# A graph layer on one core: what the scatters of a slot wait for

## The chip, the core and the metric

The kernel runs on one core of a Trainium2 chip. The core has five engines with an instruction stream each: TensorE (PE in the profile; PEld is its weight load), VectorE (DVE), ScalarE (ACT), GpSimd (POOL) and SyncE (SP). They work in order, each on its own stream, and wait for one another by semaphores. Sixteen DMA engines move data between the device memory and the on-chip memories; SP and POOL issue nearly all of this kernel's transfers.

The metric is the time of one execution on the device, in microseconds (us). The kernel before takes 1373.15 us (median of three runs, 1372.46 to 1373.16).

## The reference

There are 6250 nodes with 128 features each and 100,000 edges, sorted by their `dst` node. Each edge builds a message from its two nodes and its own features, the messages are summed at the edge's `src` node, and the result is added to the node and normalized:

```python
def layer(x, edge_index, edge_attr, W, b, gamma, beta):
    row, col = edge_index[0], edge_index[1]          # src, dst
    msg_in = concatenate([x[row], x[col], edge_attr], axis=-1)
    h = msg_in @ W + b
    mu = mean(h, axis=-1, keepdims=True)
    var = mean(square(h - mu), axis=-1, keepdims=True)
    h = (h - mu) * rsqrt(var + 1e-05) * gamma + beta
    msg = relu(h)
    return segment_sum(msg, row, num_segments=x.shape[0])
x = layernorm(x + layer(x, stack([src, dst]), edge_attr_128, W, b, gamma, beta))
```

Edges come sorted by `dst`, and are summed by `src`. The kernel therefore has to reorder them.

## The kernel before, in words

**Tiles, slots and splits.** The edges are cut into 782 tiles of 128. Four tiles make a slot, so there are 196 slots (`q`). The tiles are also cut into five splits (`SPLITS`), of 164, 168, 168, 164 and 118 tiles. The nodes are cut into 50 blocks by `src`, two of which make a pair: 25 pairs per split.

**The first half of the work: a slot.** `edges` (L520 to L534) makes four products of edge features with their part of `W` in float32 (`hp<-w,eT`, L529) and adds the `dst` node's part by four products with a one-hot matrix (`hp<-win,ohd`, L533). `evict` copies the result from PSUM to one of eight row buffers `hs` on ScalarE (L541, L542). `scatters` (L548 to L571) then sends the rows of each tile to a place in device memory by an indirect DMA from GpSimd (L559), such that the rows of one node block lie together (`sorted`). The places come from `places`, a counting sort on VectorE and TensorE (L372 to L444), worked some slots ahead.

**The second half: a pair.** When a split has been scattered, its pairs are loaded (`hl<-sorted`, L612) and go through a chain: one-hot of the block's node on VectorE (`ohe`, L630), its transposes on TensorE (L642), eviction on ScalarE (`ohn`, L646), the `src` node's part by products (`sel`, L669) on top of what ScalarE seeded (L652), squares and root on ScalarE (L678, L681), reciprocal and scaling on VectorE (L687, L693), the sum by node as float32 products (`pa`, L702), and the addition to the accumulator on VectorE (L710).

**Order.** The streams of TensorE, VectorE, ScalarE and SyncE are written out by hand: what the Python program issues first stands first. GpSimd's is left to a scheduler. The main loop goes over the slots. In a slot it issues the one-hot of slot q+2 (`edge_hot`), the products of slot q, the pair steps that are due (`work`, 100 pairs of four steps each over the slots after the first split), the eviction of slot q and the steps of `places`. The last split's pairs come after the loop (`tail`), with the final normalization.

**What paces the scatters.** In slots 13 to 194 (`TIE`), the call near the end of slot q scatters the four tiles of slot q-1 that are still in `waiting`. Each is tied to a product of slot q: `pe` has logged the products since the last call with a cost (4 for a float32 one, 1 for another), the list's total is cut in four, and the k-th scatter waits for the product in which the k-th quarter ends. Before slot 12 and after slot 194 a scatter waits for no product, only for its rows and places. All scatters go through GpSimd's queue in order, and each takes one of eight semaphores, so that it also waits for the landing of the scatter eight before it.

**Who waits for scatters.** The eviction of slot q writes the row buffer of slot q-8 and waits for that slot's four scatters to land. The pair loads of a split wait for all of its scatters. There is a second, general path behind a flag, for inputs of another shape; it isn't taken here.

## Time and profile before

| what | value |
|---|---|
| median of three runs | 1373.15 us |
| the profiled execution's own time | 1371.87 us |
| its span in the trace | 1370.07 us |
| mean granted TensorE clock | 0.857 |
| TensorE busy | 962.5 us (70%) |
| VectorE busy | 876.2 us (64%) |
| GpSimd busy | 839.3 us (61%) |
| ScalarE busy | 731.1 us (53%) |
| first and last scatter (L559) start | 24.6 us, 1224.1 us |

How to read it: busy time counts the instructions of an engine that do work, not its waits. The chain of waits follows the execution back from its last instruction, and books each stretch to the engine that was then being waited for; an engine with a small share of the chain can be busy and still not set the end. "issue" is time in which nothing that the profile shows was being waited for, and "remote" is a wait whose releaser isn't seen. The ends of TensorE's products are modelled, so a wait for one can seem to end after the product did. [...]

### The profile page before, as it was taken

What the parts mean: (1) busy time and instruction counts of PE and PEld (TensorE: products, weight loads), DVE (VectorE), ACT (ScalarE), POOL (GpSimd) and SP (SyncE); (2) the same over time, 40 slices, a digit from 0 to 9 for tenths busy, and PEclk for the clock granted to TensorE, in tenths of its full rate; (3) what the DMA queues carried; (4) which work ended last, traced back from release to release, by engine and by line L of the source; (5) the groups of instructions that cost most, each with busy time, mean ns of one, the idle gap of its engine ahead of it and who ended that gap; (6) DMA issues with size and microseconds to landing.
All of it is one profiled execution on the core that took longest, in us unless ns stands there. A gap on an engine that the chain in (4) does not pass through costs nothing.

```text
span 1370.1 us, 27285 instructions
## 1 busy us (share of the span) xinstructions
PE 962.5 (70%) x8721; PEld 857.8 (63%) x8721; DVE 876.2 (64%) x2411; ACT 731.1 (53%) x3054; POOL 839.3 (61%) x899
## 2 busy tenths in 40 slices
PE   3645555245777777777778676776877888878995
PEld 3545544235766676666667676676767777767884
DVE  8764543425566565757676665657567766657996
ACT  1222221114565555555655556555655788777996
POOL 3666667666666666666666666666666666550664
PEclk9767776566989888999998889879899999999998
DMA  6867764355656654657655554667645665532552
GB/s 199 239 200 226 223 211 145 126 169 176 204 181 209 201 172 144 189 183 217 202 183 177 182 167 157 215 192 214 212 143 183 191 187 191 168 112 92 158 162 74
DMA packets 122273, 245.78 MB, mean 179 GB/s; under 512 B 46555, under 2 KB 60396, under 8 KB 122118
## 3 DMA queue, kind: packets, MB, share of 16 engines
q1 hardware_dynamic: 95956, 189.83, 46.0%
q0 software_dynamic: 25184, 53.31, 11.0%
q8 instruction: 70, 1.15, 0.3%
q10 hardware_dynamic: 978, 0.80, 0.2%
q14 instruction: 85, 0.70, 0.2%
HBM read 155.74 MB, written 88.11 MB: 178 GB/s over the span
## 4 chain that ended last, share of the span: by engine, by line
PE 45%; issue 19%; DVE 15%; ACT 12%; another core or an unknown queue 7%; DMA 2%; POOL 0%; ACTq 0%; DVEq 0%; POOLq 0%
PE pa L702 12%; PE hp L529 12%; PE sel L669 11%; ACT sq L678 4%; PE tr L642 3%; PE hp L533 3%; DVE sc L389 3%; PE beside L426 3%; DVE msg L693 2%; DVE ohe L630 2%; ACT ohn L646 2%; ACT sel L652 2%; ACT fsq L748 1%; ACT hs L541 1%
## 5 line engine op out<-in xcount | busy, mean ns | idle before, releaser
L559 POOL DMA_INDIRECT sorted<-hs,place_i x782 | 771.8, 987 | 434.7 <-issue 196.5
L529 PE MATMUL hp<-w,eT 128*128 128x128 f32 x1564 | 276.3, 321 | 80.9 <-issue 59.1
L678 ACT ACTIVATE sq<-sel 128x128 f32<-128x128 f32 x875 | 230.8, 280 | 178.8 <-remote 62.7
L541 ACT COPY hs<-hp 128x512 f32<-128x512 f32 x196 | 114.3, 583 | 358.5 <-issue 143.5
L669 PE MATMUL sel<-xa,ohn 128*128 128x128 bf16 x2625 | 217.2, 231 | 124.2 <-issue 65.2
L702 PE MATMUL pa<-msg,ohe 128*128 128x130 f32 x1900 | 281.5, 299 | 30.5 <-issue 24.0
L669 PEld LDWEIGHTS <-ohn 128*128 128x128 bf16 x2850 | 194.0, 103 | 166.1 <-issue 150.2
L529 PEld LDWEIGHTS hp<-w,eT 128*128 128x128 f32 x1564 | 238.6, 227 | 94.5 <-issue 71.2
L702 PEld LDWEIGHTS pa<-msg,ohe 128*128 128x128 f32 x1900 | 254.7, 210 | 43.9 <-issue 36.9
L693 DVE SCALAR_TENSOR_TENSOR msg<-sel,rstd,cut 128x128 f32<-128x128 f32 x875 | 247.1, 345 | 8.7
L678 ACT ACTIVATION_READ_ACCUMULATOR sq<-sel 128x1 f32 x875 | 183.9, 210 | 0.0
L630 DVE TENSOR_TENSOR ohe<-hl,beside 128x1024 f32<-128x1024 f32 (+1 forms) x125 | 144.5, 1156 | 50.1 <-remote 19.0
L646 ACT COPY ohn<-tr 128x1024 bf16<-128x1024 bf16 (+1 forms) x125 | 120.1, 961 | 27.8 <-remote 11.1
L710 DVE TENSOR_TENSOR acc<-acc,pa 128x260 f32<-128x260 f32 x100 | 42.3, 423 | 138.5 <-remote 44.9
L517 DVE TENSOR_SCALAR ohd<-db,part_w 128x512 bf16<-128x512 bf16 x194 | 70.3, 363 | 85.2 <-remote 53.6
L652 ACT COPY sel<-hl 128x512 f32<-128x512 f32 x200 | 118.8, 594 | 1.5 <-DVE msg L693 1.5
L533 PE MATMUL hp<-win,ohd 126*128 126x128 bf16 x782 | 93.4, 241 | 29.8 <-issue 28.2
L642 PE MATMUL tr<-ident_h,ohe 128*128 128x128 bf16 x950 | 84.0, 228 | 31.4 <-issue 28.5
L533 PEld LDWEIGHTS <-ohd 126*128 126x128 bf16 x782 | 71.1, 111 | 41.3 <-issue 36.7
L642 PEld LDWEIGHTS <-ohe 128*128 128x128 bf16 x950 | 63.7, 102 | 38.7 <-issue 38.0
L687 DVE RECIPROCAL rstd<-std 128x4 f32<-128x4 f32 (+1 forms) x250 | 43.0, 172 | 65.8 <-ACT std L681 46.4
L681 ACT ACTIVATE std<-ss,eps 128x4 f32<-128x4 f32 (+1 forms) x250 | 74.4, 298 | 8.1
(159 smaller groups left out, 874.6 us busy)
## 6 DMA issues: line engine op xcount, KB each, us to landing
hl<-sorted SPq DMA_DIRECT2D x100, 528.0 KB
eT<-in_eT SPq DMA_DIRECT2D x96, 512.0 KB
sorted<-empty SPq DMA_DIRECT2D x125, 198.0 KB
db<-drel_d SPq DMA_DIRECT2D x96, 256.0 KB
sorted<-hs,place_i POOLq DMA_INDIRECT x782
hl<-sorted SPq DMA_DIRECT2D x25, 396.0 KB
win<-xb_d SPq DMA_DIRECT2D x196, 31.5 KB
xb_d<-xb SPq DMA_DIRECT2D x16, 384.0 KB
```

The lines of the kernel that those rows point to most:

```text
L529: pe(nc.tensor.matmul(hp[:, j, :], eT[:, at], w[:, 2, :], start=j == 0, stop=False, skip_group_check=True), 4)
L533: pe(nc.tensor.matmul(hp[:, j, :], oh[:3 * WN, at], win[:3 * WN, :], start=False, stop=j == m - 1, skip_group_check=True))
L541: nc.scalar.copy(hs[:, :m, 0:D], hp[:, :m, :])
L559: i = nc.gpsimd.indirect_dma_start(out=sorted_d[s][:, :], out_offset=bass.IndirectOffsetOnAxis(ap=place_i[:parts, t:t + 1], axis=0), in_=h ...
L630: nc.vector.tensor_tensor(self.ohe[:, :k, :], self.hl[:, :k, D:D + 1].to_broadcast([P, k, P]), row_bc(iota_p, k), op=ALU.is_equal)
L642: pe(nc.tensor.transpose(tr[:, j, :], half[:, j0 + j, 1::2], ident_h))
L646: nc.scalar.copy(self.ohn[:, :self.k, :], self.tr[:, :self.k, :])
L652: nc.scalar.copy(self.sel[g][:, :m, :], self.hl[:, j0:j0 + m, 0:D])
L669: pe(nc.tensor.matmul(sel[:, j, :], self.ohn[:, j0 + j, :], xa[:, b, i * D:(i + 1) * D], start=False, stop=j == m - 1 and i == 2, skip_gro ...
L678: nc.scalar.activation(sq[:, j, :], self.sel[g][:, j, :], AF.Square, accum_out=ss[:, j:j + 1])
L693: nc.vector.scalar_tensor_tensor(self.msg[:, j0 + j, 0:D], self.sel[g][:, j, :], rstd[:, j:j + 1], cut, op0=ALU.mult, op1=ALU.max)
L702: pe(nc.tensor.matmul(self.pa[:, h, :], self.ohe[:, j, :], self.msg[:, j, :], start=(j == h), stop=(j == k - 2 + h)), 4)
```

## The change

The ties keep their slots (13 to 194), their number (four) and the rows that they hold. What they hold them for changes. The log `done` no longer takes products with their cost; it takes every operation issued on VectorE, whichever step it belongs to, with a cost of its output columns plus 64. The k-th scatter of a call waits for the VectorE operation in which the k-th quarter of that total ends. To log them, all of the main path's VectorE operations are issued through a wrapper, `vec`, in place of `nc.vector`, and the products lose their `pe(...)`. Apart from the waits and signals, each engine's stream has the same instructions, and the four that are ordered by hand have them in the same order; on GpSimd, whose order the program's scheduler sets, five of the last ten scatters (those of the tiles of slots 193 and 194) change places.

```diff
     done = []
 
-    def pe(i, cost=1):
-        done.append((i.ins, cost))
-        return i
+    class Logged:
+        def __getattr__(self, name):
+            op = getattr(nc.vector, name)
+
+            def call(*args, **kw):
+                i = op(*args, **kw)
+                n = 1
+                for x in (kw["out"] if "out" in kw else args[0]).shape[1:]:
+                    n *= x
+                done.append((i.ins, n + 64))
+                return i
+
+            return call
+
+    vec = Logged()
...
         for j in range(m):
             at = slice(j * P, (j + 1) * P)
-            pe(nc.tensor.matmul(hp[:, j, :], eT[:, at], w[:, 2, :], start=j == 0, stop=False,
-                                skip_group_check=True), 4)
+            nc.tensor.matmul(hp[:, j, :], eT[:, at], w[:, 2, :], start=j == 0, stop=False,
+                             skip_group_check=True)
...
             if tied:
-                tc.add_manual_dep(i.ins, at[k].name, written, reason="rows behind products")
+                tc.add_manual_dep(i.ins, at[k].name, written, reason="rows behind VectorE's work")
...
-                nc.vector.scalar_tensor_tensor(self.msg[:, j0 + j, 0:D], self.sel[g][:, j, :],
+                vec.scalar_tensor_tensor(self.msg[:, j0 + j, 0:D], self.sel[g][:, j, :],
                                                rstd[:, j:j + 1], cut, op0=ALU.mult, op1=ALU.max)
...
-                nc.vector.tensor_tensor(acc[:, b:b + 2, :], acc[:, b:b + 2, :], self.pa,
+                vec.tensor_tensor(acc[:, b:b + 2, :], acc[:, b:b + 2, :], self.pa,
                                         op=ALU.add)
...
```

The lines left out are the same replacement, `vec` for `nc.vector` or a product without `pe`.

## The prediction, made before the changed kernel ran

> **What bounds the kernel now.** I read the page first: busy shares, chain, the groups of GpSimd and of the lines around it.

> ```profile
> PE 962.5 (70%) x8721; PEld 857.8 (63%) x8721; DVE 876.2 (64%) x2411; ACT 731.1 (53%) x3054; POOL 839.3 (61%) x899
> ...
> PE 45%; issue 19%; DVE 15%; ACT 12%; another core or an unknown queue 7%; DMA 2%; POOL 0%; ACTq 0%; DVEq 0%; POOLq 0%
> ...
> L559 POOL DMA_INDIRECT sorted<-hs,place_i x782 | 771.8, 987 | 434.7 <-issue 196.5
> ...
> L693 DVE SCALAR_TENSOR_TENSOR msg<-sel,rstd,cut 128x128 f32<-128x128 f32 x875 | 247.1, 345 | 8.7
> ```

> The scatters (L559) are 782 instructions of 987 ns, with 434.7 us of idle time before them. GpSimd holds 0% of the chain that ended last; it is TensorE, time that no shown wait explains, VectorE and ScalarE. The busy time by stage says where the scatters' engine has room:

> ```profile
> 320.00:560.00 240.00, 175.20 (x1608) 157.68 (x1607) 149.32 (x387) 133.76 (x561) 151.85 (x156) 0.85 0.60 188
> ...
> 800.00:1060.00 260.00, 195.15 (x1814) 177.05 (x1811) 170.65 (x440) 149.16 (x625) 164.51 (x169) 0.88 0.59 187
> 1060.00:1230.00 170.00, 135.21 (x1485) 126.27 (x1484) 111.63 (x337) 130.44 (x567) 103.17 (x106) 0.96 0.54 169
> ```

> Columns are the stretch, its length, busy time of PE, PEld, DVE, ACT and POOL, then TensorE's granted clock, DMA share and GB/s. From 320 to 560 us, 156 scatters at 0.97 us plus the 0.30 us that stands before even a back-to-back one need 198 of 240 us. So GpSimd has about a sixth of each slot to spare, and spends it on waits, listed here from 320 to 1230 us (line, releaser, total us, times, longest):

> ```profile
> POOL sorted L559 <- issue: 124.7, 371, 2.0
> POOL sorted L559 <- PE sel L669: 57.5, 56, 2.7
> POOL sorted L559 <- remote: 51.4, 39, 2.8
> POOL sorted L559 <- PE pa L702: 39.2, 39, 2.5
> ```

> The first row is mostly the 0.30 us (371 x 0.30 = 111 us). Taking 0.30 us off every start leaves 160 us in 182 waits after the 180th scatter. These are the ties to TensorE that the change removes.

> **What could make a scatter's time matter.** Three things wait for scatters. (a) The eviction (L541) reuses one of eight row buffers. I took each eviction's waits from the built program and the landing of those scatters from the DMA packets: the rows had left the buffer at least 23 us before the eviction started, in the median 35 us. (b) The pair loads of a finished split (L612). The last scatter of splits 0 to 3 lands 14.4, 18.4, 18.9 and 12.7 us before the first load is issued, by the same packets. (c) The last split, the tightest:

> ```profile
> 1224.11 0.87 POOL L559 DMA_INDIRECT sorted<-hs,place_i  x1 [0.30 <-issue]
> ...
> 1229.32 0.58 ACT L652 COPY sel<-hl 128x512 f32<-128x512 f32 x1
> ...
> 1229.92 0.32 SPq L612 DMA_DIRECT2D hl<-sorted  x1
> ```

> The last scatter lands at 1225.8. The load goes at 1229.92, just after ScalarE's copy out of its buffer ends at 1229.90, so it waits for the buffer. 4.1 us are spare, and its first reader (ohe, L630) runs at 1247.0.

> **The change part by part.**

> *Removed: ties of 728 scatters to products.* Of the 160 us of waits, none lies on the end's path by (a) to (c). Credit 0. If the cover were gone, the end would move by what the last scatter moves, at most.

> *Added: 605 scatters wait for a VectorE operation, 133 have no wait of their own.* One big operation (scan, one-hot) can hold two or more of the four quarter points. Behind a waiting scatter stand only the next scatters and, in the tail, the y operations; VectorE itself waits for no scatter except through a later split. Example, GpSimd first, then VectorE:

> ```profile
> 631.91 0.97 POOL L559 DMA_INDIRECT sorted<-hs,place_i  x1 [0.30 <-issue]
> 634.05 0.97 POOL L559 DMA_INDIRECT sorted<-hs,place_i  x1 [1.17 <-PE pa L702]
> 635.32 0.97 POOL L559 DMA_INDIRECT sorted<-hs,place_i  x1 [0.30 <-issue]
> 637.47 0.97 POOL L559 DMA_INDIRECT sorted<-hs,place_i  x1 [1.18 <-PE sel L669]
> ```

> ```profile
> 627.63 2.33 DVE L389 TENSOR_TENSOR_SCAN sc<-oh,beside 128x1050 bf16<-128x1050 bf16 x1
> 630.88 1.13 DVE L693 SCALAR_TENSOR_TENSOR msg<-sel,rstd,cut 128x128 f32<-128x128 f32 x4
> 633.94 0.42 DVE L710 TENSOR_TENSOR acc<-acc,pa 128x260 f32<-128x260 f32 x1 [1.93 <-PE pa L702]
> ```

> By the built program the scatter at 634.05 will wait for the scan that ended at 629.96, the next for the first L693 (631.23), the one at 637.47 for L710 (634.36). They could have gone at 633.2 (631.91 + 1.27), 634.5 and 635.7: 0.9 to 1.8 us earlier. I did this for all tied scatters, with VectorE's times as they stand and 0.25 us from release to start. After the 180th scatter the named operation had ended 2.8 us before the scatter's actual start in the median (5th and 95th percentiles 5.6 and 0.2 us); replayed in order, scatters start 1.5 us earlier in the median, never more than 2.1 us later, the last one 0.7 us earlier. GpSimd's waits come to 179 us in 168 places: the slack is moved, not removed. On the end's path: 0.7 us less of the 4.1 us spare in (c), which nobody waits for. Term 0; bounds -0.7 and 0 by this path alone.

> *Before about 320 us* neither kind of tie binds: GpSimd runs back to back behind the evictions. Term 0.

> *Signals.* TensorE instructions that signal fall from 1552 to 996; VectorE's rise from 1763 to 1855. Between 320 and 1215 us, start to start after an L693 is 258 ns without and 263 ns with a signal: 92 x 5 ns = +0.5 us if all were on the path. After an L669 product it is 56 ns either way: 556 x 0 = 0. [...]

> *GpSimd beside VectorE.* A scatter released by the end of one VectorE operation starts beside the next. 40 of 782 scatters lasted over 1.05 us, 14.2 us too long in all; of 28 that met the two-input L411, 14 are among them. If ten times as many met it, 142 us would still fit the 160 us of spare waits: term 0. [...]

> *Unknown: the phase between scatters and the rest of the DMA traffic.* TensorE has idle time with no releaser: 60.4 + 24.8 + 17.0 + 16.7 + 13.4 + 6.9 = 139.2 us "issue" from 320 to 1060 us. In microseconds where TensorE paused over 0.5 us so, 2.4 scatter packets were in flight against 1.8 otherwise, a weak link that may run either way. A scatter without a wait of its own can run on while TensorE pauses: 133 of 728, 18%, so at most 18% x 139 = 25 us lost. The other end: starts 1.5 us earlier taking as much off. I take 0, since the two kernels issue the same bytes at nearly the same mean spacing, and keep -12 and +13 (half of each) for the range.

> **Sum.** Profiled execution 1371.87 (span 1370.07 and 1.80 around it) + 0.5 = 1372.4. The median of the three runs stands 1.28 above that execution: 1373.6 us.

> **The rivals.**

> *Slower: scatters run on through TensorE's pauses.* Place: 320 to 1060 us. For it: the 139 us of unexplained pauses, the packet counts, and the ties to products stopping GpSimd exactly in such pauses (57.5 + 39.2 us of its waits). Against: VectorE starves in the same pauses a little later, and holds scatters then. Price 13 us: 1386. It decides from 2.7 us, which is 2% more pauses.

> *Faster: earlier landings release evictions.* The waits list has this row:

> ```profile
> ACT hs L541 <- DMA sorted<-hs,place_i: 42.4, 17, 5.0
> ```

> If these 17 waits were for landings, 1.5 us each would give 25 us, of which I price half as being on the chain: 12 us, 1361. Against: the program's evictions wait for scatters eight slots back, landed 23 us or more before; the last releaser seen is then a coincidence, and the product is the real one. [...]

> *No change in the order at all:* excluded as far as the program goes, since 605 waits differ; elsewhere every instruction keeps its place on its engine, but for five of the last ten scatters, which change places among themselves.

> **How the numbers follow.** Three runs span 0.7 us; 0.2% (2.7 us) is about what a measurement of this kernel tells from no change. No measurable change 0.40 (1371 to 1376), the slower rival 0.37, faster 0.23. The likeliest case's own range is 1371 to 1376. Eight in ten needs most of both rivals, whose prices are half of their bounds: 1362 to 1388 leaves out the outer tail of each, about 0.1 and 0.1. Point 1373.6.

> **What would show it.** Right: GpSimd's waits before scatters named after VectorE, about 160 to 190 us; scatters 1 to 2 us nearer to their slot; the last scatter at 1223 to 1226; busy times of all engines unchanged to 1%; the first load of the last split right after a ScalarE copy. Wrong: TensorE's "issue" time away from 139 us by over 3 us in that stretch, scatters lengthened far beyond 14 us in all, or an eviction that truly waits for a landing.

## The result, and the profile after

| | before | changed |
|---|---|---|
| median of four runs on the same chip | 1372.93 us (1372.46 to 1373.16) | 1482.7 us (1478.1 to 1490.2) |
| ratio, 95% interval | | 1.0805 (1.0756 to 1.0855) |
| span of the profiled execution | 1370.1 us | 1476.3 us |
| mean granted TensorE clock | 0.857 | 0.802 |

The change made the kernel 8% slower; 1373.6 us was forecast, within 1362 to 1388. These are lines of the changed kernel's page that answer to those shown of before: busy time, the granted clock in 40 slices, the chain that ended last, the scatters and ScalarE's squares. (Line numbers have moved by 14; L573 is the scatter. VectorE's operations all stand at L104, the wrapper's line.)

```profile
PE 1012.8 (69%) x8721; PEld 899.3 (61%) x8721; DVE 873.6 (59%) x2411; ACT 728.7 (49%) x3054; POOL 833.1 (56%) x899
...
PEclk9867676667777878786878888887787898988998
...
PE 42%; issue 21%; DVE 14%; ACT 11%; another core or an unknown queue 9%; POOL 1%; DMA 1%; SPq 0%; ACTq 0%; POOLq 0%; DVEq 0%
...
L573 POOL DMA_INDIRECT sorted<-hs,place_i x782 | 765.8, 979 | 547.0 <-issue 215.4
...
L692 ACT ACTIVATE sq<-sel 128x128 f32<-128x128 f32 x875 | 230.0, 280 | 241.0 <-remote 160.3
```

VectorE, ScalarE and GpSimd do the same work in the same time (within 1%). TensorE has the same 8721 products, but is busy 50 us longer, at a lower clock. GpSimd's share of the chain is 1%: late scatters are not what the others wait for. The stages show that the loss is everywhere in the loop (columns as in the prediction):

```profile
320.00:560.00 240.00, 165.16 (x1380) 146.12 (x1380) 131.42 (x337) 114.90 (x479) 134.87 (x139) 0.76 0.54 167
...
800.00:1060.00 260.00, 184.44 (x1642) 165.36 (x1641) 154.87 (x401) 133.77 (x569) 150.01 (x155) 0.82 0.54 169
```

In the same 240 us from 320 on, TensorE did 1380 products instead of 1608, at a clock of 0.76 instead of 0.85. What TensorE waited for, from 320 to 1060 us (line, releaser, total us, times, longest): before,

```profile
PE sel L669 <- issue: 60.4, 89, 1.9
PE tr L642 <- issue: 24.8, 32, 1.5
...
PE pa L702 <- issue: 16.7, 30, 1.1
```

and after:

```profile
PE sel L683 <- issue: 92.0, 119, 1.8
PE pa L716 <- issue: 38.8, 60, 1.7
PE tr L656 <- issue: 22.2, 34, 1.4
```

"issue" is time in which nothing that the profile shows was waited for. I call these **pauses**: over 0.25 us between two products of which the second waits for no semaphore. To compare kernels I take the loop by its work, from the first `sel` product to the last `hp` product, and split its length into pauses, waits, and the rest, which is TensorE working:

| us | loop | pauses | waits | rest | of the loop at half clock (0.5 in the trace's records of the granted clock) |
|---|---|---|---|---|---|
| before | 1037.0 | 135.9 | 90.7 | 810.4 | 204.8 |
| changed | 1139.5 | 215.1 | 65.5 | 858.8 | 389.1 |
| difference | +102.5 | +79.2 | -25.2 | +48.4 | +184.3 |

The loop explains 102.5 of the 106.2 us between the spans; the part before it is 3.9 us longer. So the loss is 79 us more pauses and 48 us of the same products run more slowly, less 25 us of waits. This count looks at the product's own waits; the weight load just ahead of it may still wait for a semaphore. Pauses where the weight load waits for nothing either I call **strict**: they are 124.6 us before and 198.9 us after, 74.3 us more.

GpSimd's waits after, from 320 to 1340 us, are named as forecast, and are longer because everything is:

```profile
POOL sorted L573 <- issue: 165.4, 408, 8.0
POOL sorted L573 <- DVE ohd L104: 120.4, 54, 6.3
POOL sorted L573 <- ACT hs L556: 35.2, 18, 4.2
POOL sorted L573 <- DVE rstd L104: 35.0, 33, 4.5
```

**One burst of pauses in each kernel.** Pauses come in bursts. In the timeline (start, length, engine, line, operation, count, idle time before it) this is one of before, TensorE first and GpSimd below:

```profile
380.87 0.61 PE L669 MATMUL sel<-xa,ohn 128*128 128x128 bf16 x5 [0.25 <-issue]
381.97 0.27 PE L669 MATMUL sel<-xa,ohn 128*128 128x128 bf16 x2 [0.49 <-issue]
383.38 0.27 PE L669 MATMUL sel<-xa,ohn 128*128 128x128 bf16 x2 [1.14 <-issue]
384.11 0.22 PE L669 MATMUL sel<-xa,ohn 128*128 128x128 bf16 x1 [0.45 <-issue]
384.81 0.27 PE L669 MATMUL sel<-xa,ohn 128*128 128x128 bf16 x2 [0.49 <-issue]
```

```profile
380.26 0.97 POOL L559 DMA_INDIRECT sorted<-hs,place_i  x1 [0.30 <-issue]
381.54 0.97 POOL L559 DMA_INDIRECT sorted<-hs,place_i  x1 [0.30 <-issue]
382.81 0.97 POOL L559 DMA_INDIRECT sorted<-hs,place_i  x1 [0.30 <-issue]
385.59 0.97 POOL L559 DMA_INDIRECT sorted<-hs,place_i  x1 [1.81 <-ACT hs L542]
```

and this one of the changed kernel:

```profile
494.68 0.22 PE L683 MATMUL sel<-xa,ohn 128*128 128x128 bf16 x1 [0.25 <-issue]
496.28 0.22 PE L683 MATMUL sel<-xa,ohn 128*128 128x128 bf16 x1 [1.39 <-issue]
497.69 0.22 PE L683 MATMUL sel<-xa,ohn 128*128 128x128 bf16 x1 [1.19 <-issue]
499.11 0.27 PE L683 MATMUL sel<-xa,ohn 128*128 128x128 bf16 x1 [1.20 <-issue]
500.51 0.27 PE L683 MATMUL sel<-xa,ohn 128*128 128x128 bf16 x1 [1.13 <-issue]
501.23 0.28 PE L683 MATMUL sel<-xa,ohn 128*128 128x128 bf16 x1 [0.46 <-issue]
502.64 0.28 PE L683 MATMUL sel<-xa,ohn 128*128 128x128 bf16 x1 [1.13 <-issue]
503.34 0.71 PE L683 MATMUL sel<-xa,ohn 128*128 128x128 bf16 x5 [0.42 <-issue]
```

```profile
494.02 0.97 POOL L573 DMA_INDIRECT sorted<-hs,place_i  x1 [0.30 <-issue]
495.29 0.96 POOL L573 DMA_INDIRECT sorted<-hs,place_i  x1 [0.30 <-issue]
496.56 1.03 POOL L573 DMA_INDIRECT sorted<-hs,place_i  x1 [0.30 <-issue]
497.90 0.96 POOL L573 DMA_INDIRECT sorted<-hs,place_i  x1 [0.30 <-issue]
499.17 0.97 POOL L573 DMA_INDIRECT sorted<-hs,place_i  x1 [0.31 <-issue]
500.44 0.97 POOL L573 DMA_INDIRECT sorted<-hs,place_i  x1 [0.30 <-issue]
504.32 0.97 POOL L573 DMA_INDIRECT sorted<-hs,place_i  x1 [2.91 <-DVE ohd L104]
```

Products of one accumulation group, which wait for nothing that the profile shows, come one or two at a time, 0.7 or 1.4 us apart, instead of every 56 ns (the median from one `sel` product to the next at full clock). Before, three scatters went out and the fourth started 1.81 us late, 0.8 us after TensorE was running again (the profile names ScalarE's L542 as what ended that wait). After, six scatters follow one another at GpSimd's shortest distance of 0.30 us until 501.41, in a burst of 8.7 us; the next waits until 504.32. The last pauses of the two bursts end 1.0 and 1.9 us after GpSimd had made its last scatter. Between 330 and 1060 us, GpSimd was making a scatter in 50% of the pause time before and in 68% after (at full clock; outside pauses 66% and 64%). Over all pauses of the loop, at either clock, it was 46% and 61%.

### The profile page after: what moved, and what is told of

The parts are those of the page before. It is cut to its first block, busy times and chain, and to the rows that moved or that the text cites. A ratio compares the mean times of both kernels' runs of the same rounds, so it can differ in the third digit from the quotient of the medians.

```text
span 1476.3 us, 27152 instructions
## 1 busy us (share of the span) xinstructions
PE 1012.8 (69%) x8721; PEld 899.3 (61%) x8721; DVE 873.6 (59%) x2411; ACT 728.7 (49%) x3054; POOL 833.1 (56%) x899
## 4 chain that ended last, share of the span: by engine, by line
PE 42%; issue 21%; DVE 14%; ACT 11%; another core or an unknown queue 9%; POOL 1%; DMA 1%; SPq 0%; ACTq 0%; POOLq 0%; DVEq 0%
PE pa L716 12%; PE hp L543 10%; PE sel L683 9%; ACT sq L692 4%; DVE sc L104 3%; PE tr L656 3%; PE hp L547 3%; PE beside L440 3%; DVE msg L104 2%; DVE ohe L104 2%; ACT ohn L660 2%; ACT sel L666 2%; PE sel L344 1%; ACT fsq L762 1%
## 5 line engine op out<-in xcount | busy, mean ns | idle before, releaser
L573 POOL DMA_INDIRECT sorted<-hs,place_i x782 | 765.8, 979 | 547.0 <-issue 215.4
L543 PE MATMUL hp<-w,eT 128*128 128x128 f32 x1564 | 284.2, 331 | 101.8 <-issue 63.0
L716 PE MATMUL pa<-msg,ohe 128*128 128x130 f32 x1900 | 303.7, 310 | 67.3 <-issue 61.6
L683 PE MATMUL sel<-xa,ohn 128*128 128x128 bf16 x2625 | 234.2, 238 | 143.8 <-issue 103.7
L716 PEld LDWEIGHTS pa<-msg,ohe 128*128 128x128 f32 x1900 | 270.5, 218 | 83.5 <-issue 74.3
L683 PEld LDWEIGHTS <-ohn 128*128 128x128 bf16 x2850 | 202.9, 106 | 193.1 <-issue 179.9
L543 PEld LDWEIGHTS hp<-w,eT 128*128 128x128 f32 x1564 | 249.6, 238 | 113.8 <-issue 72.2
L104 DVE SCALAR_TENSOR_TENSOR msg<-sel,rstd,cut 128x128 f32<-128x128 f32 x875 | 247.1, 345 | 8.6
L104 DVE TENSOR_TENSOR ohe<-hl,beside 128x1024 f32<-128x1024 f32 (+1 forms) x125 | 144.3, 1155 | 42.1 <-PE beside L440 16.6
L104 DVE TENSOR_TENSOR acc<-acc,pa 128x260 f32<-128x260 f32 x100 | 42.1, 421 | 170.8 <-PE pa L716 64.3
L104 DVE TENSOR_SCALAR ohd<-db,part_w 128x512 bf16<-128x512 bf16 x194 | 69.1, 356 | 110.2 <-remote 90.1
L656 PE MATMUL tr<-ident_h,ohe 128*128 128x128 bf16 x950 | 90.2, 237 | 26.8 <-issue 26.8
L104 DVE RECIPROCAL rstd<-std 128x4 f32<-128x4 f32 (+1 forms) x250 | 42.7, 171 | 103.5 <-ACT std L695 88.5
L656 PEld LDWEIGHTS <-ohe 128*128 128x128 bf16 x950 | 68.3, 107 | 31.4 <-issue 31.3
L695 ACT ACTIVATE std<-ss,eps 128x4 f32<-128x4 f32 (+1 forms) x250 | 74.3, 297 | 8.1
```

The lines of the kernel that those rows point to most:

```text
L104: i = op(*args, **kw)
L543: nc.tensor.matmul(hp[:, j, :], eT[:, at], w[:, 2, :], start=j == 0, stop=False, skip_group_check=True)
L573: i = nc.gpsimd.indirect_dma_start(out=sorted_d[s][:, :], out_offset=bass.IndirectOffsetOnAxis(ap=place_i[:parts, t:t + 1], axis=0), in_=h ...
L656: nc.tensor.transpose(tr[:, j, :], half[:, j0 + j, 1::2], ident_h)
L683: nc.tensor.matmul(sel[:, j, :], self.ohn[:, j0 + j, :], xa[:, b, i * D:(i + 1) * D], start=False, stop=j == m - 1 and i == 2, skip_group_ ...
L695: nc.scalar.activation(std[:, :m], ss[:, :m], AF.Sqrt, bias=eps, scale=1.0 / D)
```

## The experiments

All kernels but e10 to e12, which leave scatters out, compute the whole result. Each ratio is against the kernel before on the same chip. In e1 to e8 and e13 to e15 the log of products is back beside VectorE's (`at_pe` and `at` are the four points in either), `old_pe` is the list of the slot before, and only the list that the k-th scatter waits for differs:

```diff
             if tied:
-                tc.add_manual_dep(i.ins, at[k].name, written, ...)
+                for t_ in ties(k):
+                    tc.add_manual_dep(i.ins, t_.name, written, ...)
```

| ties(k) | ratio (95% interval) | pauses in the loop, us | half clock in the loop, us | GpSimd at a scatter in pauses (330 to 1060 us, full clock) | spread of the scatters' intervals |
|---|---|---|---|---|---|
| before: `[at_pe[k]]` | 1 | 136 | 205 | 50% | 0.29 |
| e13, the same, one slot later | 1.0004 (0.9986 to 1.0021) | 135 | 222 | 54% | 0.29 |
| e8, products at 1/8, 3/8, 5/8, 7/8 | 1.0030 (1.0018 to 1.0043) | 146 | 254 | 55% | 0.33 |
| e1 `[at_pe[k], at[k]]` | 1.0079 (1.0039 to 1.0120) | 138 | 243 | 57% | 0.34 |
| e4 `[old_pe[k]]` | 1.0165 (1.0117 to 1.0213) | 162 | 257 | 54% | 0.36 |
| e15, bf16 products alone counted | 1.0247 (1.0216 to 1.0279) | 175 | 287 | 62% | 0.42 |
| e7, `[at_pe[3]]` for the fourth alone | 1.0260 (1.0228 to 1.0293) | 179 | 304 | 62% | 0.42 |
| e14, f32 products alone counted | 1.0268 (1.0231 to 1.0304) | 153 | 281 | 69% | 0.45 |
| e5, ScalarE's operations | 1.0475 (1.0444 to 1.0506) | 197 | 321 | 61% | 0.49 |
| e6, VectorE's that read products | 1.0584 (1.0544 to 1.0623) | 210 | 352 | 65% | 0.60 |
| e3 `[]` | 1.0693 (1.0627 to 1.0759) | 227 | 369 | 72% | 0.65 |
| e2 `[at[k], old_pe[k]]` | 1.0788 (1.0736 to 1.0839) | 216 | 386 | 69% | 0.57 |
| the change: `[at[k]]` | 1.0805 (1.0756 to 1.0855) | 215 | 389 | 68% | 0.60 |

The last column is the standard deviation of the time from one scatter's start to the next in the loop, as a share of its mean: small where scatters come evenly.

### What was lost: the ties to products, their signals, or harm from the new ties (e1 to e4)

Theory A was that the pace set by TensorE's products is lost; B, that fewer signals from TensorE do it; C, that a wait for VectorE itself does harm.

> Each tied scatter waits for the product of before and for the VectorE operation of the change. Theory A (the pace that the ties to products give is what was lost): near the kernel before, 1370 to 1395 us. Theory B (TensorE signals 556 times less often in the changed kernel, and that costs): near before too, since the signals are back. Theory C (waiting for VectorE does harm of itself, by its signals or by its late releases): near the changed kernel, 1450 to 1490 us.

> The changed kernel, and each tied scatter also waits for the product of the slot before its own, which is long done: TensorE signals 1479 times in place of 997, and no scatter moves. Theory A: as the changed kernel, 1470 to 1490 us. Theory B: back near before, 1370 to 1395 us. Theory C: as the changed kernel.

> No ties: a scatter waits for its rows and places alone. Theory A: as slow as the changed kernel or slower, 1470 us or more, since nothing holds a scatter in TensorE's pauses. Theory B: as the changed kernel, 1470 to 1490 us, since TensorE's signals are as few (997). Theory C: near before, 1365 to 1390 us.

> Each tied scatter waits for the product at its quarter of the slot before, which is long done: TensorE's 1551 signals without their pace, no waits for VectorE. Theory A: as without ties, 1470 us or more. Theory B: near before, 1370 to 1395 us. Theory C: near before, 1365 to 1390 us.

e1 took 1387.5 us, e2 1484.0, e3 1470.9, e4 1398.3 (before on that chip: 1374.6). e2 has 482 of the 556 lost signals back (1478 in place of 996) and is as slow as the change: B falls. e3 waits for no VectorE operation and has nearly the whole loss: C alone falls, and what a tie to VectorE adds on top of another pace or of none is about 1% (e1 over before; the change over e3). Only where it comes later than a tie to a product and so takes its place does it cost more: e2 is 6% over e4. So of the ties before, about 96 us (e3 against before) were gain, and VectorE's give none of it. e4 is what made it hard, for A expected 1470 us or more of it: its scatters start nearly as soon after their eviction as those of e3 (3.9 and 3.5 us in the mean), about half of GpSimd's waits are for the rows' own eviction (89 of 187 us after the 180th scatter), and yet it is 73 us faster than e3. How early a scatter goes is therefore not the point. But e4's ties are not to products "long done", as its expectation says: products end 53 us of those waits, and a releaser that isn't seen another 40 us. So a part of the hold by TensorE is left in e4.

### Which tie holds, and where (e5 to e8)

The four share a new theory F and two rivals, G and H. (The pauses in their expectations are those of the whole execution, some 100 to 130 us above those of the loop.) e5 logs ScalarE's operations from `evict` to `square`, with a cost of their columns plus 200. e6 logs for the ties only what `scale` and `add` issue on VectorE. For e7 and e8:

```diff
+    def ties(k):                      # e7
+        return [at_pe[k]] if k == 3 else []
-            while len(at) < n and seen * n >= (len(at) + 1) * total:
+            while len(at) < n and seen * n >= (len(at) + 0.5) * total:    # e8, products
```

> The four scatters of a slot wait for ScalarE's operations of the next slot at the four even parts (by columns), with nothing tied to TensorE's products. ScalarE's squares, evictions and copies read what TensorE has just made, so they stop with it. Theory F (TensorE has bursts of pauses that no wait explains; scatters that may start inside a burst prolong it; a tie is worth what it holds back inside a burst): 1370 to 1415 us, TensorE's pauses without a wait 215 to 265 us, GpSimd at scatters in under 0.6 of the pause time. Theory G (only a wait for TensorE's own signal does it): 1465 to 1490 us, pauses about 330 us. Theory H (any tie to another engine is as bad as VectorE's): the same as G.

> As the changed kernel, the scatters wait for VectorE, but only its operations that read products out of PSUM (msg, acc) are counted for the four parts, where the slot has any; the scans, one-hots and row masks, which run ahead of TensorE, are not. Theory F: the scatters then stop when TensorE stops, so most of the loss comes back: 1385 to 1430 us, pauses 230 to 280 us. Theory G, and Theory H (waiting for VectorE is the harm, whatever operation): 1465 to 1490 us, pauses 315 to 340 us.

> Only the fourth scatter of a slot waits for a product (the last of the next slot); the other three have no tie. Theory F: the queue is held once a slot, so that scatters can get at most one slot ahead of TensorE; a burst that falls in the three free scatters' time is prolonged still: 1395 to 1440 us, pauses 255 to 295 us. Theory G: a quarter of the gain, about 1445 us. If only the even spacing of all four counts: 1460 to 1475 us as without ties.

> As the kernel before, but the four products are those at 1/8, 3/8, 5/8 and 7/8 of the slot's work in place of 1/4 to 4/4, so each scatter may go half a part earlier. Theory F: the hold is the same, 1365 to 1390 us, pauses 210 to 240 us. If the exact place in the slot counts (a phase against the loads): anything from 1360 to 1440 us, with pauses that follow it.

They took 1453.0, 1473.0, 1427.2 and 1393.2 us, with 1390.0 for before on this chip (some 15 us more than on the first, so the ratios are what counts). The times of e7 and e8 came out as F said; the pauses of the whole execution were 295 us in e7, at the end of F's range, and 264 us in e8, above its 240. e7 shows that one held scatter in four is worth 60% of the gain, not a quarter (1.0260 of 1 to 1.0693). e5 and e6 missed F: operations that read the products recover a third and a sixth of the loss, where F had most of it. F's condition for e5, GpSimd at a scatter in under 60% of the pause time, was missed by the table's count (61%) and met over all pauses of the loop (52%), so it decides nothing. H and G fall with e5, whose 1.0475 is well under the 1.065 that they asked for.

### Do the scatters make the pauses? (e9 to e12)

No ties here. So that scatters can be left out without reading rows that nothing wrote, the clearing of `sorted` covers all rows from split 1 on:

```diff
         _, k, f, _ = SPLITS[s]
+        f = f if s == 0 else 0
...
         for k, (s, q, j) in enumerate(waiting[:n]):
+            if tied and s:
+                continue                                     # e10
+                nc.gpsimd.memset(idle_t, 0.0)                # e11, then continue
+                nc.sync.dma_start(rows_d[t * P:(t + 1) * P, :],
+                                  hs_all[q % HS][:, j, :])   # e12, then continue
```

> The control for the next three. No ties at all, and for splits 1 to 4 the clearing of a pair's rows writes all its rows and not only those that may stay empty (+33 MB written by SP's queue), so that scatters can be left out beside it without reading unwritten rows. Every theory: about as without ties, 1460 to 1500 us, TensorE's pauses without a wait 320 to 360 us.

> As the control, but the scatters of splits 1 to 4 are left out (about 618 of 782; rows of those splits stay empty). The instructions of TensorE, VectorE and ScalarE are the same. Theory F (scatters in TensorE's bursts prolong them): 1290 to 1360 us, pauses 100 to 200 us. If the bursts have another cause (pair loads, code loading) and scatters are only beside them: 1440 to 1500 us, pauses over 300 us.

> As the last, but in the place of each scatter left out GpSimd clears a buffer of its own (128x1056 f32, 968 ns in the profile of before against 987 ns of a scatter), released by the same eviction: GpSimd's work without the transfer. If the transfer of the rows is what prolongs the bursts: as without scatters, 1290 to 1360 us, pauses 100 to 200 us. If GpSimd's running is: 1440 to 1500 us.

> As without scatters, but in the place of each scatter left out SP's queue writes the same 128 rows of 528 bytes from the same buffer to a place of their own, one after the other: the transfer without GpSimd's indices, not tied to TensorE. If the transfer of the rows is what prolongs the bursts: 1400 to 1500 us, pauses over 250 us. If it takes GpSimd's indirect form: as without scatters, 1290 to 1370 us, pauses 100 to 200 us.

| | ratio (95% interval) | loop, us | pauses, us | strict pauses, us | half clock, us |
|---|---|---|---|---|---|
| e9, control | 1.0693 (1.0639 to 1.0746) | 1135.6 | 219.7 | 203.2 | 370.9 |
| e10, no scatters | 0.7685 (0.7647 to 0.7722) | 752.7 | 3.8 | 0.0 | 37.5 |
| e11, memsets in their place | 0.7929 (0.7890 to 0.7968) | 786.6 | 10.4 | 0.0 | 58.0 |
| e12, plain writes of the rows | 0.8845 (0.8782 to 0.8908) | 905.6 | 31.9 | 1.0 | 129.7 |

This settles that the pauses need the scatters. With 612 of the 782 gone, TensorE's pauses in the loop fall from 220 us to 4, and the strict ones from 203 to none, though the pair loads and edge loads and all products are there. The chain, a window and what TensorE waited for from 320 to 1000 us in e10:

```profile
DVE 41%; PE 21%; ACT 14%; issue 8%; POOL 4%; another core or an unknown queue 3%; DMA 2%; SPq 0%; ACTq 0%; DVEq 0%; POOLq 0%
```

```profile
320.00:560.00 240.00, 216.53 (x2490) 208.71 (x2488) 225.29 (x594) 196.88 (x841) 0.00 (x0) 0.98 0.80 276
```

```profile
PE beside L421 <- DVE cnt L104: 33.4, 12, 3.9
PE sel L703 <- ACT sel L686: 15.8, 28, 2.2
```

No "issue" row is left in that list, the clock is 0.98, and VectorE, 94% busy, has become the bound. F expected 1290 to 1360 us and, in the whole execution, 100 to 200 us of pauses; 1067.5 us and 93 us show that it was far too timid on the time. The scatters cost this kernel some 420 us untied and 320 us as before has them, while their own waits gate nothing. GpSimd's being busy isn't it: e11 keeps it busy with a memset of 986 ns for each scatter left out, and has no strict pause. Nor is it the load on the DMA engines, as one window of e9 and then of e12 shows:

```profile
320.00:560.00 240.00, 164.62 (x1431) 148.00 (x1429) 134.57 (x340) 117.05 (x492) 136.66 (x141) 0.79 0.61 206
```

```profile
320.00:560.00 240.00, 183.29 (x1912) 171.33 (x1911) 175.30 (x458) 154.34 (x651) 0.00 (x0) 0.92 0.84 253
```

e12 moves the same 276 MB as e9, with the DMA engines busier (0.84 against 0.61 here), and has 1 us of strict pauses: the other 31 us of its count stand behind weight loads that wait for a semaphore. Its time of 1228.6 us can't be read as a price of pauses, since DMA holds 26% of its chain. So the pauses need the indirect form of the scatters: what GpSimd does in the 979 ns of each (987 before), or the transfers as its queue does them, to scattered places (they go on after it: the changed kernel's last scatter left GpSimd at 1330.7 us, and its rows landed at 1331.5). No run leaves out one and keeps the other. What the traces show of it is a coincidence in time only: in the changed kernel's loop, strict pauses took 11% of the time with neither, 16% while GpSimd made a scatter and no scatter packet was in flight, 23% with packets in flight alone, and 29% with both (before: 10, 8, 24 and 12%). Loading of code (queues 8 and 14, of kind `instruction`) is not it: its packets were in flight in 6% of the changed kernel's loop and in 2% of its strict pauses (queue 8; 2% and 2% for queue 14). What stops TensorE no trace shows.

### Hold, age, or neighbours (e13 to e15)

```diff
-                scatters(len(waiting) - PT, True)
+                scatters(max(0, len(waiting) - 2 * PT), True)     # e13
+        if (cost == 4) == True:        # e14; False in e15, in pe()
             done_pe.append((i.ins, cost))
```

> As the kernel before (ties to TensorE's products at the four even parts), but the scatters of a slot are issued one slot later, so they wait for the products of the slot after the next. Theory F (a scatter does harm where it starts in a burst of TensorE's pauses, and a tie to a product keeps it out): the hold is the same or tighter, since nothing else than the product can be the last to release it: 0.985 to 1.005 of before, GpSimd at scatters in at most half of the pause time. If the scatters' age or their place against the loads counts: over 1.01, as with the ties one slot earlier (1.0165).

> As the kernel before, but only the slow f32 products (hp from eT, pa) are counted for the four parts, so every scatter is released at the end of an f32 product and mostly runs beside f32 products. Theory F alone: 0.99 to 1.02 of before. If besides the hold it counts which products a scatter runs beside (pauses stood in 12% and 10% of the time of hp and pa in the loop of before, in 24% and 29% of that of sel and tr): 0.96 to 0.99.

> The counterpart: only the bf16 products (hp from the rows' windows, tr, sel) are counted, so every scatter is released at the end of a bf16 product. Theory F alone: 0.99 to 1.02 of before. If it counts which products a scatter runs beside: 1.02 to 1.05.

They took 1374.0, 1407.6 and 1405.5 us, with 1372.7 for before. One slot later changes nothing that can be measured, so age isn't it (GpSimd was at a scatter in 54% of the pause time, where F had at most half). Scatters released by f32 products alone are no better than those released by bf16 products alone: the kind of neighbour isn't it either, and the expectation for f32 falls. Both are 2.5% slower than the even four parts, a little more than F allowed. What they share is that their scatters come less evenly: the spread of the intervals is 0.45 and 0.42, against 0.29 before. The share of scatters in pauses, which puts the other kernels nearly in the order of their times, fails for e14 (69% at 1.0268). The spread of the intervals does not: it puts all thirteen kernels nearly in the order of their ratios, e5 and e14 among them. So there is a rival to the hold by TensorE, that even spacing by itself keeps the pauses down. No run spaces the scatters evenly without TensorE's products, and pauses may themselves bunch the scatters, so this stays untested.

**Where this leaves the cause.** Shown: the pauses need the indirect scatters, and neither a busy GpSimd nor the same rows written by SP's queue makes them; ties to products keep the pauses at 135 to 180 us, even one in four, unless a later tie to VectorE takes their place (e2); ties to VectorE's or ScalarE's operations, or none, leave 197 to 227 us. Argued, not shown: that the tie works because scatters stop when TensorE does, so that a burst ends by itself. The timelines speak for it; e14's share and the poor showing of e5 speak against it as the whole account. Open: whether it is that hold or the even spacing that counts, and the mechanism in the hardware.

## Why the prediction was wrong, point by point

- **Scatters are off the end's path as events: right.** After, the rows had left a buffer at least 25 us before the eviction that reuses it. The last split's first load went at 1336.6 us, 5.1 us after the last scatter landed at 1331.5 (4.1 us before). "Term 0" was right for this path, and it was not the path that mattered.
- **Removed ties, credit 0: wrong, and the step that failed** together with the next. The 160 us of waits that looked like pure slack had a use: e3, which only drops them, is 6.9% slower.
- **The phase between scatters and the other traffic, taken as 0 with bounds -12 and +13: wrong, by the size.** The slower rival named the mechanism and the place: scatters run on through TensorE's pauses, 320 to 1060 us. It was priced at 18% of the 139 us of "issue", by the 133 scatters left without a wait, and halved. Two premises of that price failed. The pauses were treated as given and only stretched; e10 shows that there are none without the scatters (strict pauses 203 us to 0). The reason given for 0, nearly the same mean spacing, held no better: what changed is how evenly the scatters come, with intervals that spread by 0.60 of their mean and not by 0.29. And only scatters with no wait were counted; with a wait for VectorE they run on as well, for the scatters were in 68% of the pause time and not in 50%. The six "issue" rows that summed to 139.2 us sum to 183.3.
- **"VectorE starves in the same pauses a little later, and holds scatters then": wrong.** Even ties to just the VectorE operations that read products (e6) recover only a sixth of the loss. The replay gives a likely reason: the named operation had ended 2.8 us before the scatter in the median, so at the start of a burst about two scatters, at 1.27 us each, are already released.
- **The granted clock was left out of the sum.** It carries +48 us of the 102.5: the products themselves, at half clock for 389 us of the loop instead of 205.
- **Scatters' own times: right in kind.** The start after the end of the eviction fell from 8.7 to 7.4 us in the mean (forecast: 1.5 us earlier in the median); 165 waits longer than the 0.30 us after the 180th scatter (forecast 168), but 267 us of them and not 179, since the slots are longer.
- **Signals, +0.5 us: right within the measurement.** e2 returns 482 of the 556 signals and stays at 1.0788.
- **GpSimd beside VectorE, term 0: right.** The mean scatter went from 987 to 979 ns; 31 lasted over 1.05 us, where 40 had.
- **Before 320 us, term 0: nearly right**, +3.9 us.
- **The range**: it ended at 1388 because both bounds of the unknown were worked out as fractions of what the profile of before showed, and before was the kernel in which this cost was kept small.

## What to carry to other kernels

A wait that gates nothing can still be worth 7% (e3, 1.0693): ask of it not only who waits for the waiting instruction, but which transfers it keeps apart from which engine. Where a profile has idle time that no wait explains, price it first by leaving the suspected traffic out altogether, since a fraction of the idle time seen is no bound for what it becomes: here 13 us were priced, and the pauses grew by 79 us. Count the clock as a second loss beside the pauses of TensorE: here the same products took 48 us more beside those 79.
